# Bias row sums, operand loads further ahead and a denser row order in a two-layer graph kernel

## The chip, the cores and the metric

The kernel runs on one core of one Trainium2 chip. The metric is the device time of one execution in microseconds. A profiled execution, taken by the hardware profiler, shows where that time goes; inside it, times are counted from the start of its span. All matrix work is in 32-bit floats, and the trace shows every such matmul as two records: a 128x512 matmul is two records that start 0.43 us apart.

## The reference

N is 4096 nodes, D is 512 features, H is 128 hidden features. The first layer is attention with the adjacency matrix added twice to the scores, a residual and a layer norm; the second is a two-layer graph convolution with a residual and a layer norm.

```python
q = x @ Wq.T + bq;  k = x @ Wk.T + bk;  v = x @ Wv.T + bv
a = q @ k.T / sqrt(D) + adj + adj
x = layernorm(x + softmax(a) @ v)
h = relu(adj @ (x @ W1) + b1)
out = layernorm(x + adj @ (h @ W2) + b2)
```

The biases bq, bk, bv, b1 and b2 are not zero.

## The kernel before

All five engines run one instruction stream each, in the order in which the Python code calls them. The order is written out by hand; waits come from data dependences and from buffers that are used again. DMAs are issued by SyncE (SP), ScalarE (ACT) and GpSimd (POOL), each from its own in-order queue.

**Head** (lines 608 to 677). q k^T is computed as x M x^T plus bias terms, where M is Wq^T Wk times a scale. The head loads the transposed weights (wq_t on ACT's queue, wk_t on SP's), turns them back with TensorE transposes (psw), and computes M (psm). The bias terms are matmuls too: bk spread over 128 columns (bk_b) times Wq gives g_t in every row (psg); bk_b times bq gives the constant c0_t (psc); Wk times bq, one column at a time, gives ub_t (psub). Then row_parts computes one number per node, the sum of x times g, as a VectorE multiply with a running sum, and add_c0 adds the constant. The helpers spread (put a column on a diagonal, VectorE) and in_every_row (a matmul of ones with that diagonal, then a copy by ACT) turn a column into a row that stands in all 128 partitions. u_products (psu) multiplies M with x^T, and its result plus ub_t is the right operand of the scores.

**Row stages.** Queries are taken in NG = 8 groups of 512 columns. The unit loop issues, for each group g, the score products (qk, lines 346 and following, by a seven-product Strassen scheme) and, woven between them, a list of further work: for the group before it, the products P x (px_items, line 482, again seven products per block, each a *phase*) and, for the group before that, the rows (row_items): rows_out multiplies with Wv, adds the residual and starts the layer norm; rows_norm applies it on ACT; add_b2 adds b2 on POOL into a tile xb and stores it to x1_d; project turns the row tile (x1ps, copied to x1t), and project2 multiplies it with W1 (tps). Every gap between two score products takes items from the list until its share of the time is used up. The last group's P x has no scores beside it.

Each phase needs a left operand from x (plain parts, from the input) or from xs_d (sums that were stored before); load_x fetches it on SP into one of three buffers of the pool xnp. It is called at the start of phase n for phase n + 2. SP also loads the score operands (load_s), into the pool sap of eight buffers, which the xb tiles of add_b2 share.

**Second layer.** adj times the node features runs in four Strassen blocks (b, line 851, its right operands prepared by VectorE from the adjacency tiles ck), then a plain product for the last 1024 columns in three parts of 512, 256 and 256 (acce, line 1123). Adjacency tiles are loaded by SP (load_to, line 792), up to ten tiles ahead in the last part. During the last block and the parts, out_row finishes output rows: a matmul with W2 (ops), an addition of the x1 row (xp, loaded in pairs by load_pair on ACT's queue, two pairs ahead, four buffers), a layer norm, and a store on ACT's queue.

Of the kernel before, what the change touches and what calls it, by code (L numbers as in the profile page):

```python
# [24 lines left out]
def tile_graph_attention_then_gcn(  # L25
# [380 lines left out]

    def load_x(n):
        g, a, b, k = PHASES[n]
        XN[n] = xnp.tile([P, b - a, 2 * P], F32, tag="xn", name=f"xn{n}")
        plain = {1: (0, 0), 2: (1, 0), 4: (1, 1)}  # L410
        if k in plain:
            t, f = plain[k]
            src = x.rearrange("(d t j p) f -> t p d j f", p=P, t=2, j=2)[t]
            for d in range(a // 2, b // 2):
                nc.sync.dma_start(
                    XN[n][:, 2 * d - a : 2 * d - a + 2], src[:, d, :, ts(f, 2 * P)]
                )
        else:
            nc.sync.dma_start(XN[n], xs_d[a][:, {6: 0, 7: 1, 3: 2, 5: 3}[k]])
# [47 lines left out]
    def px_items(g):  # L467
        def one(n, q, f):
            _, a, b, k = PHASES[n]

            def go():
                if q == a and f == 0:
                    if n + 2 < len(PHASES):
                        load_x(n + 2)
                    if k in (6, 5, 3, 4):
                        read_px(("PY",) if k == 4 else ("PX",))
                    if k == 1 and a == 0:
                        OT[g] = rowp.tile([P, ND, W], F32, tag="ot", name=f"ot{g}")
                    if k in (1, 2, 7):
                        T["PX" if k == 1 else "PY"] = bank("o", f"p{n}", 4)  # L480
                begins = k in (1, 2, 7) and q == a
                nc.tensor.matmul(  # L482
                    T["PX" if k in (1, 6, 5, 3) else "PY"][:, ts(f, HW)],
                    XN[n][:, q - a, ts(f, P)],
                    quarters(g, q)[{1: 0, 2: 2, 6: 1, 7: 0, 5: 1, 4: 2, 3: 3}[k]],
                    start=begins and f == 0,
                    stop=q == b - 1,
                    skip_group_check=True,
                )
                if f == 1:  # L490
                    if k == 6:
                        px_t34(g, q)
                    if k == 7:
                        px_t1(g, q)
                    if q == b - 1:
                        px_read(g, a == 0, k)

            return PX_US, go

        return [  # L500
            one(n, q, f)
            for n, (g_, a, b, k) in enumerate(PHASES)
            if g_ == g
            for q in range(a, b)
            for f in range(2)
        ]
# [74 lines left out]
    def row_items(g, between):  # L581

        def item(us, f, *args):
            return us, lambda: f(*args)

        def out(r):
            return [item(0.86, rows_out, g, r, c) for c in range(ND)]

        def norm(r):
            return [item(0, rows_norm, g, r), item(0, add_b2, g, r)]

        def pro(r):
            return [item(0.44, project, g, r)]

        def pro2(r):
            return [item(0.9, project2, g, r)]

        w = between  # L600
        return [
            *out(0), *out(1), *out(2), *norm(0), *out(3), *norm(1), *w(4), *norm(2), *pro(0),
            *w(8), *norm(3), *pro(1), *pro2(0), *w(8), *pro(2), *pro2(1), *w(8), *pro(3),
            *pro2(2), *w(8), *pro2(3),
        ]


    with tc.tile_pool(name="wqk", bufs=1) as wp:
        wk_t = wp.tile([P, ND, D], F32, name="wk_t")
        wq_t = wp.tile([P, ND, D], F32, name="wq_t")  # L610
        wk_n = wp.tile([P, ND, D], F32, name="wk_n")
        wq_n = wp.tile([P, ND, D], F32, name="wq_n")
        bk_b = wp.tile([P, ND, P], F32, name="bk_b")

        nc.scalar.dma_start(wq_t, wqT.rearrange("(c p) o -> p c o", p=P))
        nc.sync.dma_start(wk_t, wkT.rearrange("(c p) o -> p c o", p=P))
        make_identity(nc, ident)
        nc.gpsimd.memset(ones, 1.0)
        nc.gpsimd.memset(half_t, -0.5)
        nc.scalar.dma_start(bq_t, bq)  # L620
        nc.scalar.dma_start(bk_t, bk)
        load_xts(0)
        rows0 = t_sb[:, : PER * PER, :].rearrange("p (r a) b -> p r (a b)", r=PER)
        nc.sync.dma_start(rows0, x[:W, :].rearrange("(r p) d -> p r d", p=P))
        load_xts(1)
        for i in range(4):
            nc.gpsimd.dma_start(
                b1_t[ts(i // 2, H // 2), i % 2 : i % 2 + 1], b1[ts(i % 2, H // 2), :]
            )
        for o in range(ND):  # L630
            nc.vector.tensor_scalar(bk_b[:, o, :], ones, bk_t[:, o : o + 1], None, ALU.mult)

        def evict(n, out_, in_):
            if n % 2:
                nc.vector.tensor_copy(out_, in_)
            else:
                nc.scalar.copy(out_, in_)


        for w_t, w_n in ((wq_t, wq_n), (wk_t, wk_n)):  # L640
            for o in range(ND):
                ps = bank("o", f"psw{o}", 4)
                for c in range(ND):
                    nc.tensor.transpose(ps[:, ts(c, P)], w_t[:, c, ts(o, P)], ident)
                evict(o, w_n[:, o, :], ps)
        ps = mbank("psg")
        for o in range(ND):
            nc.tensor.matmul(ps, bk_b[:, o, :], wq_n[:, o, :], start=o == 0, stop=o == ND - 1)
        nc.vector.tensor_scalar(g_t, ps, HALF_SCALE, None, ALU.mult)

        for a in range(ND):
            ps = bank("o", f"psm{a}", 4)
            for o in range(ND):
                nc.tensor.matmul(
                    ps, wq_n[:, o, ts(a, P)], wk_n[:, o, :], start=o == 0, stop=o == ND - 1
                )
            evict(a, m_t[:, a, :], ps)
        ps = mbank("psc")
        for o in range(ND):
            nc.tensor.matmul(  # L660
                ps[:, :1], bk_b[:, o, :], bq_t[:, o : o + 1], start=o == 0, stop=o == ND - 1
            )
        nc.vector.tensor_scalar(c0_t, ps[:, :1], HALF_SCALE, None, ALU.mult)
        ps = mbank("psub")
        for a in range(ND):
            for o in range(ND):
                nc.tensor.matmul(
                    ps[:, a : a + 1],
                    wk_n[:, o, ts(a, P)],
                    bq_t[:, o : o + 1],  # L670
                    start=o == 0,
                    stop=o == ND - 1,
                )
        nc.vector.tensor_scalar(ub_t, ps[:, :ND], HALF_SCALE, None, ALU.mult)
        for r in range(PER):
            row_parts(r, rows0[:, r, :])
        add_c0(0)

    SLOTS = 12

# [242 lines left out]
    for g in range(NG):  # L923
# [30 lines left out]
                px.insert(40 + 29 * n, (0.86, lambda u=u, k=k: product(u, k)))  # L954
        if g:
            px.reverse()
            items = row_items(g - 1, lambda n: [px.pop() for _ in range(n)])
            work[s1 + 1] = NP, items + px[::-1]
        else:
            work[s1 + 3] = NP - 2, px  # L960

    at(NP + 2, 3, load_x, 0)
    at(NP + 2, 5, load_x, 1)

    last_unit = (NG + 1) * NP + 1
    at(last_unit - 5, 0, lambda: [sum_t(0, 0, 8), sum_t(8, 8, 14)])
# [6 lines left out]
    for unit in range(last_unit):  # L973
        if unit == NP + 2:
# [4 lines left out]
            wv_t = wvp.tile([P, ND, D], F32, name="wv_t")  # L979
            w1_t = wvp.tile([P, ND, H], F32, name="w1_t")  # L980
            rowp = att.enter_context(tc.tile_pool(name="rows", bufs=1, side="right"))
        if unit == NP + 6:
            nc.sync.dma_start(wv_t, wvT.rearrange("(c p) o -> p c o", p=P))
            nc.sync.dma_start(w1_t, w1.rearrange("(c p) h -> p c h", p=P))
# [46 lines left out]
    def last_pools():  # L1031
        att.close()
        return [
            ctx.enter_context(tc.tile_pool(name=name, bufs=bufs, side="right"))
            for name, bufs in (("hp", 1), ("cp", 1), ("yp", 4), ("rows1", 4), ("small1", 4))
        ]

    put(61, lambda: pools.extend(last_pools()))
# [35 lines left out]
    def load_pair(i):  # L1074
        if i < NT // 2:
            XP[i] = rowp.tile([P, 2, D], F32, tag="x1", name=f"xp{i}")
            nc.scalar.dma_start(XP[i], x1_d[i])

    def out_row(uT, i):

        if i % 2 == 0:
            load_pair(i // 2 + 2)
        ps = mbank(f"ops{i}")
        nc.tensor.matmul(ps, uT, w2_t, start=True, stop=True)  # L1084
        y = XP[i // 2][:, i % 2]
# [16 lines left out]
            out_row(*pending.pop(0))  # L1102

    put(0, rows_of, 2, C[2])
    put(1, load_pair, 0)
    put(1, load_pair, 1)
    for n in range(18, 54, 6):
        put(n, some_rows, 1)
    strassen(3, beside)
# [3 lines left out]
    for n, (i0, cols, ld) in enumerate(parts):  # L1113
        acc = bank("o", f"acce{n}", 4)[:, :cols]
        per = 2048 // cols
        for j in range(NT):
            if j % (2 * per) == 0:
                load_to((ld + j // per) // 2 + 5)
            if n == 0 and j == 0:
                rows_of(3, C[3])  # L1120
            if j % (2, 5, 10)[n] == 1:
                some_rows(1)
            nc.tensor.matmul(  # L1123
                acc,
# [3 lines left out]
                stop=j == NT - 1,  # L1128
            )
        uT = yp.tile([P, cols], F32, tag="y", name=f"uTe{n}", padded_shape=[P, 1024])  # L1130
        nc.scalar.copy(uT, acc)
        pending += [(uT[:, ts(r, P)], i0 // P + r) for r in range(cols // P)]
    some_rows(len(pending))

# [42 lines left out]
```

## Time and profile before

| | |
|---|---|
| three runs | 2392.92, 2397.09 and 2399.93 us; median 2397.09 |
| profiled execution | 2397.79 us, span 2395.8 us, mean granted TensorE clock 0.994 |
| busy | PE 97%, VectorE (DVE) 66%, GpSimd (POOL) 42%, ACT 16% |
| moved | 522.98 MB, 218 GB/s on average |

Four views are used. The page gives the share of each engine. The list of waits names for an engine the line that waited, who released it, the total, the number of times and the longest. The timeline shows instructions in order of time: start, duration, engine, line, operation, out<-in, shapes, count, and in brackets the engine's idle time before it with what ended that. A table of windows gives the busy time per engine in stretches of the span, with the clock that TensorE was granted, the share of time that the DMA engines were busy, and GB/s. PEld is TensorE's weight load, which overlaps the matmuls.

### The profile page before, as it was taken

Reading aid. Unit: us, or ns where it says so; the run is one execution under the profiler, and the core shown is the slowest. Engines: PE = TensorE matmul, PEld = TensorE weight load, DVE = VectorE, ACT = ScalarE, POOL = GpSimd, SP = SyncE. Lnnn points to the kernel's source line nnn. Section 1 sums busy time; section 2 is a strip of 40 time slices with the busy share of each in tenths; the row PEclk is TensorE's granted clock in tenths of the full one; section 3 lists DMA queues with packets and bytes.
Section 4 is the critical chain, followed back from the end, with each engine's and each line's share of the span. In section 5 each row is a group of like instructions: output and inputs, shape, how many; then the busy total and the mean of one; then the engine's idle time right before and its main releaser. Section 6 shows DMA issues by size and latency. Waiting matters only on the chain.

```text
span 2395.8 us, 27767 instructions
## 1 busy us (share of the span) xinstructions
PE 2323.8 (97%) x10352; PEld 1705.7 (71%) x10352; DVE 1579.3 (66%) x2205; ACT 385.1 (16%) x398; POOL 1004.9 (42%) x1004
## 2 busy tenths in 40 slices
PE   8999899999999999999999999999998999999997
PEld 4666678878878887888788788878886743333445
DVE  2556665577568666765775576667657777888863
ACT  1111211031112112210311121121102100000012
POOL 0666554174237424541752274246429830001032
PEclk9999999999999999999999999999999999999999
DMA  4789877856766784768567667857664468999995
GB/s 140 236 266 301 243 207 189 231 159 189 206 171 179 206 220 141 206 186 230 145 196 208 171 172 199 221 151 202 181 203 153 144 233 311 332 350 333 356 384 182
DMA packets 271460, 522.98 MB, mean 218 GB/s; under 512 B 19104, under 2 KB 119968, under 8 KB 270432
## 3 DMA queue, kind: packets, MB, share of 16 engines
q1 hardware_dynamic: 223088, 404.81, 50.8%
q0 software_dynamic: 39872, 97.00, 19.2%
q10 hardware_dynamic: 8368, 19.41, 2.3%
q8 instruction: 83, 1.36, 0.2%
q14 instruction: 49, 0.40, 0.1%
HBM read 473.18 MB, written 46.40 MB: 217 GB/s over the span
## 4 chain that ended last, share of the span: by engine, by line
PE 87%; DVE 6%; DMA 3%; POOL 2%; issue 2%; ACT 0%; SPq 0%; POOLq 0%; DVEq 0%; ACTq 0%
PE p L482 29%; PE X L346 17%; PE b L851 14%; PE Y L346 13%; PE x L545 4%; PE psu L168 4%; PE acce L1123 2%; DVE s L435 2%; DVE s L440 1%; DMA xn<-in_x_dram 1%; PE ops L1084 1%; PE tps L576 1%; DVE s L359 1%; DMA ck<-in_adjT_dram 1%; DMA s<-in_adjT_dram 1%
## 5 line engine op out<-in xcount | busy, mean ns | idle before, releaser
L482 PE MATMUL p<-s,xn 128*128 128x256 f32 x3584 | 895.4, 381 | 34.5 <-DMA xn<-in_x_dram 12.1
L482 PEld LDWEIGHTS p<-s,xn 128*128 128x128 f32 x3584 | 678.4, 190 | 142.2 <-issue 13.7
L346 PE MATMUL X<-ut,sa 128*128 128x256 f32 x1984 | 515.0, 383 | 5.1 <-DVE s L359 5.1
L346 PEld LDWEIGHTS X<-ut,sa 128*128 128x128 f32 x1984 | 373.1, 191 | 108.2 <-issue 43.3
L402 POOL TENSOR_TENSOR lacc<-lacc,s 128x512 f32<-128x512 f32 x240 | 351.6, 1465 | 201.2 <-ACT s L393 191.4
L359 DVE TENSOR_TENSOR s<-X,s 128x512 f32<-128x512 f32 x256 | 176.4, 689 | 365.2 <-PE X L346 355.8
L346 PE MATMUL Y<-ut,sa 128*128 128x256 f32 x1408 | 361.0, 379 | 3.2 <-DVE s L359 1.8
L346 PEld LDWEIGHTS Y<-ut,sa 128*128 128x128 f32 x1408 | 266.3, 190 | 63.4 <-issue 25.6
L393 ACT ACTIVATE s<-s 128x1024 f32<-128x1024 f32 x128 | 135.4, 1058 | 863.4 <-DVE s L389 863.4
L292 POOL DMA_DIRECT2D s<-in_adjT_dram x64 | 86.7, 1355 | 413.7 <-ACT s L287 413.7
L359 DVE TENSOR_TENSOR s<-Y,s 128x512 f32<-128x512 f32 x192 | 132.1, 688 | 184.5 <-PE Y L346 184.4
L389 DVE TENSOR_TENSOR s<-s,mb 128x512 f32<-128x512 f32 x256 | 233.3, 917 | 0.0
L368 DVE TENSOR_TENSOR macc<-macc,s 128x512 f32<-128x512 f32 x240 | 226.6, 944 | 1.2
L526 POOL TENSOR_SCALAR rstd<-mv 128x1 f32<-128x1 f32 x64 | 26.4, 412 | 460.6 <-DVE mv L524 459.9
L455 DVE TENSOR_TENSOR ot<-p,ot 128x512 f32<-128x512 f32 x248 | 168.8, 681 | 28.6 <-PE p L482 27.8
L818 DVE TENSOR_TENSOR tt<-ck 128x1024 f32<-128x1024 f32 x112 | 138.2, 1271 | 41.6 <-PE b L851 38.8
L851 PE MATMUL b<-tt,st 128*64 128x512 f32 (+1 forms) x768 | 156.1, 541 | 0.0
L435 DVE TENSOR_TENSOR s<-s 128x512 f32<-128x512 f32 x128 | 138.5, 1104 | 2.0 <-POOL s L429 2.0
L168 PE MATMUL psu<-xt,m_t 128*128 128x512 f32 x256 | 129.7, 600 | 0.0
L545 PE MATMUL x<-wv_t,ot 128*128 128x512 f32 x256 | 124.9, 597 | 1.1 <-DVE xr L550 0.9
L287 ACT COPY s<-cb 128x2048 f32<-128x2048 f32 x64 | 120.4, 1890 | 0.6
L428 POOL TENSOR_TENSOR s<-s 128x256 f32<-128x256 f32 x128 | 119.9, 937 | 0.6
(130 smaller groups left out, 1929.3 us busy)
## 6 DMA issues: line engine op xcount, KB each, us to landing
ck<-in_adjT_dram SPq DMA_DIRECT2D x128, 1024.0 KB, 7.2
s<-in_adjT_dram POOLq DMA_DIRECT2D x64, 1024.0 KB, 11.9
sa<-s_d SPq DMA_DIRECT2D x224, 256.0 KB, 5.6
xn<-in_x_dram SPq DMA_DIRECT2D x192, 256.0 KB, 3.5
xn<-xs_d SPq DMA_DIRECT2D x96, 512.0 KB, 4.9
sa<-in_xT_dram SPq DMA_DIRECT2D x168, 256.0 KB, 4.5
xn<-xs_d SPq DMA_DIRECT2D x64, 256.0 KB, 3.9
u_d<-uo POOLq DMA_DIRECT2D x7, 1792.0 KB, 7.4
```

The source lines that it names most:

```text
L168: nc.tensor.matmul(ps[o], m_t[:, c, ts(o, P)], XTS[b][:, c, :], start=c == 0, stop=c == ND - 1)
L346: nc.tensor.matmul(T["X" if k in (1, 6, 5, 3) else "Y"][:, ts(j, HW)], SA[g, d, a][:, c, j, :], UT[g, b][:, c, :], start=k in (1, 2, 7) an ...
L359: nc.vector.tensor_tensor(ck, ps, ck, ALU.add)
L368: nc.vector.tensor_tensor(MACC[g], MACC[g], ck[:, h, :], ALU.max)
L389: nc.vector.tensor_tensor(ck, ck, MB[g], ALU.subtract)
L402: nc.gpsimd.tensor_tensor(LACC[g], LACC[g], ck[:, h, :], ALU.add)
L435: nc.vector.tensor_tensor(b, b, t2, ALU.subtract)
L455: nc.vector.tensor_tensor(to, ps, to, ALU.add)
L482: nc.tensor.matmul(T["PX" if k in (1, 6, 5, 3) else "PY"][:, ts(f, HW)], XN[n][:, q - a, ts(f, P)], quarters(g, q)[{1: 0, 2: 2, 6: 1, 7: 0 ...
L545: nc.tensor.matmul(ps, OT[g][:, c, ts(r, P)], wv_t[:, c, :], start=c == 0, stop=c == ND - 1)
L818: nc.vector.tensor_tensor(t[:, :2], v[:, :, 1], v[:, 0], ALU.subtract)
L851: nc.tensor.matmul(BK[n][k][ts(half, HH)], lhs, right(u, i, half, b), start=q == 0, stop=q == NP - 1,)
```

## The change

There are five edits.

1. In the head, bk and bq are made into rows that stand in every partition (bk_r, bq_r), by two diagonals and two broadcasts ahead of the transposes. g, ub and c0 are then sums over a row: VectorE multiplies the loaded transposed weights with such a row and accumulates (times). g is turned into a row by a further diagonal and broadcast, after the second of four M products; c0, row_parts and add_c0 follow there. psg, psc, psub and bk_b go. The weights are loaded in halves, all on SP, wq first; bk and bq are first on ACT's queue.
2. load_x is called three phases ahead instead of two, with a fourth buffer (pool xnp2) for every fourth phase.
3. row_items takes another order: normalisations one row earlier, and two P x items between rows where there were four or eight. For the last group three times as many are taken.
4. x1 pairs are loaded by SP, four pairs ahead, with six buffers.
5. In the last three parts, the first output row of a part comes some tiles later, and VectorE instead of ACT copies the accumulated result (uTe).

```diff
-        XN[n] = xnp.tile([P, b - a, 2 * P], F32, tag="xn", name=f"xn{n}")
+        pool = xnp2 if n % 4 == 3 else xnp
+        XN[n] = pool.tile([P, b - a, 2 * P], F32, tag="xn", name=f"xn{n}")
...
-                    if n + 2 < len(PHASES):
-                        load_x(n + 2)
+                    if n + 3 < len(PHASES):
+                        load_x(n + 3)
...
-            *out(0), *out(1), *out(2), *norm(0), *out(3), *norm(1), *w(4), *norm(2), *pro(0),
-            *w(8), *norm(3), *pro(1), *pro2(0), *w(8), *pro(2), *pro2(1), *w(8), *pro(3),
-            *pro2(2), *w(8), *pro2(3),
+            *out(0), *out(1), *norm(0), *out(2), *norm(1), *out(3), *norm(2), *w(2), *pro(0),
+            *norm(3), *w(2), *pro(1), *w(2), *pro2(0), *w(2), *pro(2), *w(2), *pro2(1), *w(2),
+            *pro(3), *w(2), *pro2(2), *w(4), *pro2(3),
...
-        bk_b = wp.tile([P, ND, P], F32, name="bk_b")
-        nc.scalar.dma_start(wq_t, wqT.rearrange("(c p) o -> p c o", p=P))
-        nc.sync.dma_start(wk_t, wkT.rearrange("(c p) o -> p c o", p=P))
+        bq_r = wp.tile([P, W], F32, name="bq_r")
+        bk_r = wp.tile([P, W], F32, name="bk_r")
+        g_c = wp.tile([P, ND], F32, name="g_c")
+        nc.scalar.dma_start(bk_t, bk)
+        nc.scalar.dma_start(bq_t, bq)
+        for w_t, wT in ((wq_t, wqT), (wk_t, wkT)):
+            for o in range(2):
+                nc.sync.dma_start(
+                    w_t[:, :, ts(o, D // 2)],
+                    wT.rearrange("(c p) o -> p c o", p=P)[:, :, ts(o, D // 2)],
+                )
...
-        nc.scalar.dma_start(bq_t, bq)
-        nc.scalar.dma_start(bk_t, bk)
...
-        for o in range(ND):
-            nc.vector.tensor_scalar(bk_b[:, o, :], ones, bk_t[:, o : o + 1], None, ALU.mult)
...
+        def times(w_t, b_r, into):
+            product = t_sb[:, 24 : 24 + PER, :].rearrange("p a b -> p (a b)")
+            for c in range(into.shape[1]):
+                nc.vector.scalar_tensor_tensor(
+                    product, w_t[:, c, :], HALF_SCALE, b_r, ALU.mult, ALU.mult,
+                    accum_out=into[:, c : c + 1],
+                )
+        for name, b_t, b_r in (("bk", bk_t, bk_r), ("bq", bq_t, bq_r)):
+            spread(b_t, name)
+            in_every_row(name, b_r)
...
-        ps = mbank("psg")
-        for o in range(ND):
-            nc.tensor.matmul(ps, bk_b[:, o, :], wq_n[:, o, :], start=o == 0, stop=o == ND - 1)
-        nc.vector.tensor_scalar(g_t, ps, HALF_SCALE, None, ALU.mult)
+        times(wq_t, bk_r, g_c)
+        spread(g_c, "g")
+        times(wk_t, bq_r, ub_t)
...
-        ps = mbank("psc")
-        for o in range(ND):
-            nc.tensor.matmul(
-                ps[:, :1], bk_b[:, o, :], bq_t[:, o : o + 1], start=o == 0, stop=o == ND - 1
-            )
-        nc.vector.tensor_scalar(c0_t, ps[:, :1], HALF_SCALE, None, ALU.mult)
-        ps = mbank("psub")
...
-        nc.vector.tensor_scalar(ub_t, ps[:, :ND], HALF_SCALE, None, ALU.mult)
-        for r in range(PER):
-            row_parts(r, rows0[:, r, :])
-        add_c0(0)
+            if a == 1:
+                in_every_row("g", g_t)
+                times(bq_r.unsqueeze(1), bk_r, c0_t)
+                for r in range(PER):
+                    row_parts(r, rows0[:, r, :])
+                add_c0(0)
...
-            items = row_items(g - 1, lambda n: [px.pop() for _ in range(n)])
+            by = 3 if g == NG - 1 else 1
+            items = row_items(g - 1, lambda n: [px.pop() for _ in range(n * by)])
...
-    at(NP + 2, 5, load_x, 1)
+    at(NP + 2, 4, load_x, 1)
+    at(NP + 2, 5, load_x, 2)
...
+            xnp2 = att.enter_context(tc.tile_pool(name="xnp2", bufs=1, side="right"))
...
-            for name, bufs in (("hp", 1), ("cp", 1), ("yp", 4), ("rows1", 4), ("small1", 4))
+            for name, bufs in (("hp", 1), ("cp", 1), ("yp", 4), ("rows1", 6), ("small1", 4))
...
-            nc.scalar.dma_start(XP[i], x1_d[i])
+            nc.sync.dma_start(XP[i], x1_d[i])
...
-            load_pair(i // 2 + 2)
+            load_pair(i // 2 + 4)
...
-    put(1, load_pair, 0)
-    put(1, load_pair, 1)
+    for i in range(4):
+        put(1, load_pair, i)
...
-            if j % (2, 5, 10)[n] == 1:
+            if j % (2, 5, 10)[n] == (1, 3, 4)[n]:
...
-        nc.scalar.copy(uT, acc)
+        nc.vector.tensor_copy(uT, acc)
```

More of the change, by code (lines that the diff above doesn't have):

```diff
@@ L637, in evict @@
                 nc.scalar.copy(out_, in_)
+        def times(w_t, b_r, into):
+            product = t_sb[:, 24 : 24 + PER, :].rearrange("p a b -> p (a b)")
+            for c in range(into.shape[1]):
+                nc.vector.scalar_tensor_tensor(
+                    product,
+                    w_t[:, c, :],
+                    HALF_SCALE,
+                    b_r,
+                    ALU.mult,
+                    ALU.mult,
+                    accum_out=into[:, c : c + 1],
[3 more added lines that the diff above has]
+            in_every_row(name, b_r)
         for w_t, w_n in ((wq_t, wq_n), (wk_t, wk_n)):
@@ L657, in tile_graph_attention_then_gcn @@
             evict(a, m_t[:, a, :], ps)
-        ps = mbank("psc")
-        for o in range(ND):
-            nc.tensor.matmul(
-                ps[:, :1], bk_b[:, o, :], bq_t[:, o : o + 1], start=o == 0, stop=o == ND - 1
-            )
-        nc.vector.tensor_scalar(c0_t, ps[:, :1], HALF_SCALE, None, ALU.mult)
-        ps = mbank("psub")
[L665 to L673, printed above, removed]
-        nc.vector.tensor_scalar(ub_t, ps[:, :ND], HALF_SCALE, None, ALU.mult)
-        for r in range(PER):
-            row_parts(r, rows0[:, r, :])
-        add_c0(0)
+            if a == 1:
[4 more added lines that the diff above has]
+                add_c0(0)
     SLOTS = 12
```

## The prediction

> **What bounds the kernel now.** First the busy shares and the granted clock on the page:
>
> ```profile
> span 2395.8 us, 27767 instructions
> PE 2323.8 (97%) x10352; PEld 1705.7 (71%) x10352; DVE 1579.3 (66%) x2205; ACT 385.1 (16%) x398; POOL 1004.9 (42%) x1004
> PEclk9999999999999999999999999999999999999999
> ```
>
> TensorE works 97% of the span. Work taken off VectorE or GpSimd is worth nothing by itself; only PE's instructions, or the 72 us in which PE idles, can be won. So the second view is what PE waits for:
>
> ```profile
> PE p L482 <- DMA xn<-in_x_dram: 12.1, 6, 2.7
> PE psw L644 <- DMA wq_t<-in_wqT_dram: 10.7, 1, 10.7
> PE p L482 <- DVE ot L455: 7.4, 7, 1.5
> PE ops L1084 <- DVE xp L1086: 6.3, 2, 4.4
> PE p L482 <- DVE s L435: 5.6, 5, 1.6
> PE ops L1084 <- ACT uTe L1131: 2.2, 2, 1.8
> PE p L482 <- DMA xn<-xs_d: 1.7, 2, 1.4
> ```
>
> (total, times, longest.) The third is the timeline of the start, for PE work that could go:
>
> ```profile
> 10.74 3.31 PE L644 MATMUL psw<-ident,wq_t 128*128 128x128 f32 x16 [10.74 <-DMA wq_t<-in_wqT_dram]
> 13.89 1.97 PE L644 MATMUL psw<-ident,wk_t 128*128 128x128 f32 x16
> 15.69 3.60 PE L648 MATMUL psg<-wq_n,bk_b 128*128 128x512 f32 x8
> 19.12 13.90 PE L654 MATMUL psm<-wk_n,wq_n 128*128 128x512 f32 x32
> 32.86 0.95 PE L660 MATMUL psc<-bq_t,bk_b 128*128 128x1 f32 x8
> 33.67 3.71 PE L667 MATMUL psub<-bq_t,wk_n 128*128 128x1 f32 x32
> 37.24 5.38 PE L168 MATMUL psu<-xt,m_t 128*128 128x512 f32 x8
> ```
>
> PE starts at 10.7 us, and psg, psc and psub run one after another ahead of psu. The windows show one thing more (length, then PE, PEld, DVE, ACT, POOL busy, PE clock, DMA share, GB/s):
>
> ```profile
> 33.00:37.30 4.30, 4.30 (x42) 4.30 (x40) 0.85 (x2) 0.00 (x0) 0.00 (x0) 1.00 0.00 0
> 37.30:41.30 4.00, 4.00 (x7) 1.70 (x7) 3.71 (x11) 0.00 (x0) 0.00 (x0) 0.57 0.31 68
> ```
>
> After the one-column psub the granted clock was 0.57.
>
> **Head.** Removed from PE: psg 3.44, psc and psub 4.38 (32.86 to 37.24). Added: three 128x512 broadcasts of 0.86 (the bcc row: two records, 0.43 apart), two of them ahead of the transposes. *Loads:* wq and wk now go in four halves on SP, bk and bq first on ACT. Before, wq (9.9 us to landing) shared the engines with wk; SP's four 1 MB loads landed at 9.5, 12.8, 15.3 and 17.9, 2.5 to 3.3 us apart, and the rate was 362 to 369 GB/s from 3 us on. So the 0.5 MB halves land near 4.3, 5.8, 7.4 and 9.0. A rule speaks against this: the Trainium skill, "DMA: Bandwidth & Descriptors" (Anatomy of one DMA), puts 2.0 us plus bytes at 436 GB/s on a DMA, and its Bandwidth section asks for 1 MiB each. My estimate from it, one after another: 3.2 us a half, the last at 13.5. That would start psm near 14.5 and cost 2.5 us. The trace shows loads queued on SP landing with no such gap, so I take 9.0. *Biases:* bq and bk landed 0.8 us apart behind wq; the quietest x1 load took 2.0. At the queue's front that gives about 3.6 and 4.4. The other end is the b_t row, tiny loads on a queue of their own, 6.5 us: 7.2 and 7.8. I take the former, since it is these very loads. Then the diagonal on DVE (0.69) and the broadcasts: at half clock 1.72 each, from 4.5 to 7.9. The skill's "TensorE: Matmul & The Clock Gate" (Part 1) says PE begins at half clock until some 3.4 us of activity, and falls back after as long idle. That speaks against work put at the front: full clock would give 0.86 each. The trace agrees, with 3.31 for the first 16 transposes against 1.97 for the next, so I charge the half clock; it costs 1.7 us at most. Transposes (1.73 for sixteen, the wk row) 7.9 to 9.7 and, wk being there, to 11.4; with slack, psm from 12 (11.5 to 15 by the biases' ends), plus 13.73 plus 0.86: psu at 26.6 against 37.24, so 10.6. The slow stretch goes too: the first eight psu records took 5.24 in the chain, where eight at 0.43 are 3.44: 1.8. Sum 12.4; I take **12** (9 to 13).
>
> On DVE nine row sums of 0.69 + 0.08 (the L325 rows) and three diagonals replace six small operations. Four sums and a diagonal, 3.8, must be done before the g broadcast, which stands behind two psm groups (6.9): 3 us of cover. ub (3.1) and c0 with row_parts (about 4.8) lie beside the rest of psm, whose second half is 6.9. Were that cover gone, at most 3 us would show. ACT gains three copies of 0.59 while idle.
>
> **Three ahead.** In each of six row stages PE waits once for an xn tile, 1.3 to 2.7 us. The cause stands in SP's own waits between 685 and 770 us and in its timeline there:
>
> ```profile
> SPq L254 <- DMA x_d<-xb: 11.9, 1, 11.9
> 723.24 0.32 SPq L419 DMA_DIRECT2D xn<-xs_d  x1
> 735.50 0.32 SPq L254 DMA_DIRECT2D sa<-s_d  x1
> 735.92 0.40 SPq L415 DMA_DIRECT2D xn<-in_x_dram  x1
> 739.74 0.67 PE L482 MATMUL p<-s,xn 128*128 128x256 f32 x2 [1.60 <-DMA xn<-in_x_dram]
> ```
>
> An sa load waits 12 us for a buffer that an xb row holds until its store lands, and the xn load behind it on the in-order SP queue is late. A fourth buffer puts that load one phase (3 to 6 us) earlier, ahead of the hold or with more time behind it; the denser order also brings xb forward and puts P x phases some 4 us later just there. The next load is late then, but has a phase more: landing takes 3.5, it is due about 6 us after 736. Six waits: 1.34 + 1.60 + 2.40 + 2.68 + 1.91, and 2.50 at 1403 in the same place, put down to an ACT copy long done: **12.4**. The first stage loses its 2.2 and 0.2, **2.4** (low end 0, if the copies of wv in the queue still delay it).
>
> **Denser rows** change no PE work; 18 instead of 36 P x items lie between row items, and the rest run later, all together. Costs come from tighter order. On ACT the third and fourth normalisations now come right after their matmuls and may wait for POOL; behind them stand the x1t and ot copies, on which the next transposes and phases wait, with 1.6 us (two items at the stage's pace of 1.84) of cover for a 0.59 copy. On PE, P x without rows between begins 11 us earlier. The nearest row is the stage's own rowless stretch, with one wait of 1.0 per stage (ot L455). The upper bound is stage 0, dense throughout: 1.35 + 0.83 + 1.58 = 3.8 per stage, 23 in all; below nothing, those 5.9 of ot waits and 1.9 of s waits could also vanish. I take half a wait a stage: **+3**.
>
> **Last row stage** (no QK). Its 11.5 of idle is POOL and DVE preparing P x, 1.4 is xn. Three times the items between rows leave phases at nearly the same places (k=6 due 17.6 us in, both ways), but xb of row 1 (1.27 + 0.3 + 0.67) moves ahead of the P x subtraction that PE awaits at 1812 for 2.9 us: +2. Net **+0.6** (-4 to +4).
>
> **Tail.** Two waits come from late x1 rows and one from the uTe copy:
>
> ```profile
> 2331.63 1.12 PE L1084 MATMUL ops<-w_t,y 128*128 128x512 f32 x2 [1.81 <-DVE xp L1086]
> 2345.47 0.69 DVE L1086 TENSOR_TENSOR xp<-ops,xp 128x512 f32<-128x512 f32 x1 [7.72 <-DMA xp<-x_d]
> 2346.22 2.07 PE L1084 MATMUL ops<-w_t,y 128*128 128x512 f32 x2 [4.45 <-DVE xp L1086]
> 2369.93 1.12 PE L1084 MATMUL ops<-w_t,uTe 128*128 128x512 f32 x2 [1.79 <-ACT uTe L1131]
> ```
>
> Four pairs ahead give 20.6 us (eight rows of 2.57) instead of 10.3. Now SP: a load waits for the stores of the pair six before it, and ck loads queue behind; and it queues behind ck loads that wait for slots. At the first part's start eight ck loads are issued at once, the last held until tile 7 is used, 10 us; the x1 load behind lands after some 17, in time. ck is ten tiles ahead there, so the reverse hold (2 to 3 us) is covered. The uTe copy on DVE takes 0.69 or 0.42 and the first row now stands three tiles later: 1.8 gained. Against it: 2 MB of x1 instead of 1.5 stand early in the last Strassen block, where DMA already runs at 400 GB/s and DVE waited 2.1 for ck with some 1.3 of slack to PE: 0.5 MB is 1.3 us, so I charge 1.2 (0 to 6). **6.3 + 1.8 - 1.2 = 6.9.**
>
> **Sum.** 12 + 2.4 + 12.4 - 3 - 0.6 + 6.9 = 30.1. The profiled execution took 2397.8 (its span and 2.0 around it): 2367.7. It stands 0.7 above the median of the three runs, hence **2367**.
>
> **Rivals.** *The stall moves:* dense phases and ACT's earlier waits eat the row stages' gain (9.4) and cost 2.4 more in the last: 2379. For it speaks stage 0; against it that DVE has a third of its time free. *Biases late:* psm at 15 or later, and the tail's gain halved: 2367 + 3 + 3.5 = 2374. For it speaks the b_t row. *SP's queue decides (the slower side):* in the last block ten x1 loads each wait for an out store (5.7 us to landing) and hold the ck loads behind; of these 57 us the refill at the part's start covers 10, so 47 are lost on top of 2367: 2414. It ends slower once over 3 us a load show on PE (30 won, ten loads). Against it: ck's lead, and no PE wait for ck now. *It does nothing:* each wait is followed by another of its size, 2397; against it, psg, psc and psub are PE work that is gone.
>
> **Numbers.** Likeliest 0.66, its own range 2357 to 2377; stall moves 0.17, biases 0.09, SP 0.05, nothing 0.03. Faster by over 0.3% (7.2 us; the runs span 2392.9 to 2399.9, so less is not told from no change) 0.91, within 0.04, slower 0.05. The range for 8 in 10 takes in the first rival and the bounds: 2354 to 2384.
>
> **What would show it.** psu from 25 to 30 us with no window at 0.57; no PE wait for xn above 1 us in the six stages; no wait of ops for xp; new waits of x1ps or tps, or more of ot, would be the dense rows' price. It is wrong if psm starts after 16, if p waits grow past 12 in the six stages, or if b or acce waits for ck.

## The result, and the profile after

The changed kernel took 2366.97 us (median of four runs, 2365.97 to 2367.78), the kernel before 2398.4 in its four runs beside it (2392.92 to 2399.93): a ratio of 0.9873, with a 95% interval of 0.9856 to 0.989. The predicted time was 2367. But two parts of that sum are wrong by 5.7 and by 7.0 us in opposite directions. That they cancel is luck, so the number says less for the reasoning than it seems to.

The page's first rows after. TensorE is again the engine that is nearly always busy; VectorE is busy 13 us longer than before:

```profile
span 2365.5 us, 27707 instructions
PE 2313.5 (98%) x10310; PEld 1697.6 (72%) x10310; DVE 1592.0 (67%) x2222; ACT 383.5 (16%) x398; POOL 1011.4 (43%) x1004
```

Next, from the list of TensorE's waits over the whole span after, the rows used below (waiting line and its releaser; total, times, longest):

```profile
PE p L483 <- DVE s L436: 8.1, 10, 1.9
PE ops L1094 <- DVE xp L1096: 8.1, 2, 7.5
PE X L346 <- DVE s L359: 8.0, 18, 1.0
PE bcbk L315 <- DVE diagbk L304: 4.9, 1, 4.9
PE p L483 <- POOL s L430: 3.5, 1, 3.5
...
PE p L483 <- POOL xb L560: 2.4, 1, 2.4
...
PE p L483 <- DVE ot L456: 1.5, 2, 1.0
...
PE ops L1094 <- DVE uTe L1141: 0.5, 1, 0.5
```

The wait for xn is gone, the start waits 4.9 us instead of 10.7, and the ot waits (7.4) are down to 1.5. Others have grown. ops waits for xp 7.5 us at once where the two waits before were 6.3 together. The waits for s that VectorE prepares went from 5.6 to 8.1 (p) and from 5.1 to 8.0 (X), and p has a new wait of 2.4 for xb.

To see where the time went, cut both spans at the same instructions. Every row is the distance between two first occurrences in the two timelines (first psu at 37.24 and 26.34, first score matmul at 53.61 and 40.94, the mt transpose of group 1 at 465.29 and 449.31, that of the last stage at 1785.17 and 1754.12, the first x matmul of the last group's rows at 1933.89 and 1903.94, the first acce at 2297.38 and 2268.18, the end at 2395.8 and 2365.5):

| Stretch | before | after | gain | predicted |
|---|---|---|---|---|
| head, to the first score | 53.61 | 40.94 | 12.7 | 12 |
| first stage | 411.68 | 408.37 | 3.3 | 2.4 |
| six middle row stages | 1319.88 | 1304.81 | 15.1 | 12.4 - 3 = 9.4 |
| last row stage | 148.72 | 149.82 | -1.1 | -0.6 |
| Strassen blocks to the first part | 363.49 | 364.24 | -0.8 | -1.2 |
| the parts, to the end | 98.42 | 97.32 | 1.1 | 6.3 + 1.8 = 8.1 |
| sum | | | 30.3 | 30.1 |

The head in the timeline after (start, duration, engine, line, operation, out<-in, shapes, count, idle before it and what ended that):

```profile
4.92 2.04 PE L315 MATMUL bcbk<-diagbk,ones 128*128 128x512 f32 x2 [4.92 <-DVE diagbk L304]
6.76 1.66 PE L315 MATMUL bcbq<-diagbq,ones 128*128 128x512 f32 x2
8.26 1.91 PE L666 MATMUL psw<-ident,wq_t 128*128 128x128 f32 x16
10.00 1.91 PE L666 MATMUL psw<-ident,wk_t 128*128 128x128 f32 x16
11.75 7.03 PE L675 MATMUL psm<-wk_n,wq_n 128*128 128x512 f32 x16
18.62 1.02 PE L315 MATMUL bcg<-diagg,ones 128*128 128x512 f32 x2
19.48 7.03 PE L675 MATMUL psm<-wk_n,wq_n 128*128 128x512 f32 x16
26.34 3.60 PE L168 MATMUL psu<-xt,m_t 128*128 128x512 f32 x8
```

The two broadcasts take 2.04 and 1.66 where the one for g takes 1.02: the slow first microseconds of TensorE now fall on two matmuls (four records), and the sixteen transposes behind them need 1.91 instead of 3.31. The granted clock reads 1.00 from 4.90 to 8.26 us, so this slowness shows in the durations alone. The broadcast of g stands in the middle of psm with no wait. The first eight psu records take 3.60 instead of 5.38.

The tail after, around the one long wait:

```profile
2253.77 36.26 SPq L799 DMA_DIRECT2D ck<-in_adjT_dram  x10
2290.12 4.22 SPq L1087 DMA_DIRECT2D xp<-x_d  x2
2302.11 0.69 DVE L1096 TENSOR_TENSOR xp<-ops,xp 128x512 f32<-128x512 f32 x1 [11.92 <-DMA xp<-x_d]
2302.86 2.07 PE L1094 MATMUL ops<-w_t,y 128*128 128x512 f32 x2 [7.54 <-DVE xp L1096]
```

SP issues ten ck loads over 36 us and only then comes to the next x1 pair, which lands 12 us later. TensorE stands for 7.54 us and then is slow. The windows say how slow (length; PE, PEld, DVE, ACT, POOL busy; granted clock; DMA share; GB/s):

```profile
2300.00:2302.80 2.80, 0.00 (x0) 0.00 (x0) 0.69 (x1) 0.00 (x0) 0.00 (x0) 0.50 1.04 380
2302.80:2306.20 3.40, 3.34 (x4) 1.50 (x5) 3.09 (x8) 0.81 (x1) 1.60 (x5) 0.50 1.09 349
2306.20:2310.00 3.80, 3.80 (x7) 1.57 (x6) 1.31 (x3) 1.63 (x2) 1.54 (x5) 0.68 1.06 385
```

At 0.50 and 0.68 these 7.2 us do 4.3 us of work: the wait costs 2.9 more than its own length.

### The profile page after: what moved, and what is told of

Read it like the earlier page. It is cut to its first block, busy times and chain, and to the rows that moved or that the text cites. A ratio compares the mean times of both kernels' runs of the same rounds, so it can differ in the third digit from the quotient of the medians.

```text
span 2365.5 us, 27707 instructions
## 1 busy us (share of the span) xinstructions
PE 2313.5 (98%) x10310; PEld 1697.6 (72%) x10310; DVE 1592.0 (67%) x2222; ACT 383.5 (16%) x398; POOL 1011.4 (43%) x1004
## 4 chain that ended last, share of the span: by engine, by line
PE 90%; DVE 6%; issue 1%; DMA 1%; POOL 1%; ACT 0%; DVEq 0%; POOLq 0%; ACTq 0%
PE p L483 30%; PE X L346 17%; PE b L858 14%; PE Y L346 13%; PE x L546 4%; PE psu L168 4%; PE acce L1133 2%; DVE s L436 2%; PE tps L577 1%; PE ops L1094 1%; DVE s L359 1%; DVE s L441 1%; DMA s<-in_adjT_dram 1%; PE x1ps L568 1%; PE psm L675 1%
## 5 line engine op out<-in xcount | busy, mean ns | idle before, releaser
L389 DVE TENSOR_TENSOR s<-s,mb 128x512 f32<-128x512 f32 x256 | 244.1, 957 | 0.0
L429 POOL TENSOR_TENSOR s<-s 128x256 f32<-128x256 f32 x128 | 125.4, 980 | 0.6
```

Of the source, the lines that this page charges most:

```text
L389: nc.vector.tensor_tensor(ck, ck, MB[g], ALU.subtract)
```

## The experiments

Each of the first seven takes back one part of the change, or tests one suspected cause, by itself. The runs of the kernel before that stand beside them have medians of 2396.89 (x1_act, own_xb, old_rows and xn_two) and 2396.43 (the other four), seven runs each.

**x1_act: x1 on ACT's queue, otherwise the changed kernel.**

```diff
-            nc.sync.dma_start(XP[i], x1_d[i])
+            nc.scalar.dma_start(XP[i], x1_d[i])
```

> The changed kernel, with the x1 pairs loaded by ACT's queue again, still four pairs ahead with six buffers. Theory A (the 7.5 us wait of ops at 2303 us comes from x1 loads standing on SP's in-order queue behind ten ck loads, which take 26 us at 390 GB/s): on a queue of their own they share the engines with ck and arrive in time; ops waits for xp fall below 2 us in all, 2367.0 becomes about 2360. Theory B (the DMA engines are simply full there, at 390 GB/s, whichever queue a load stands on): the wait stays at 6 to 8 us, the time within 1.5 us of 2367. A third outcome, waits of b or acce for ck, would mean that x1 takes ck's place.

Measured: 2357.62 us (2356.82 to 2358.89), ratio 0.984 (0.9823 to 0.9856). From the first acce to the end it takes 87.78 us instead of 97.32, and every other stretch stays within 1.5 us of the changed kernel's. TensorE's waits in that stretch, all of them:

```profile
PE ops L1094 <- DVE cl L875: 1.1, 1, 1.1
PE ops L1094 <- DVE uTe L1141: 0.5, 1, 0.5
```

So the four pairs' lead is worth 9.5 us more than the changed kernel got, and SP's queue is what took it away. Against the kernel before the parts gain 10.6 here: more than the 8.1 of idle time that the prediction had counted. The windows over the parts, before and then in x1_act, show where the rest is:

```profile
2297.00:2396.00 99.00, 82.23 (x250) 47.41 (x244) 41.45 (x82) 22.45 (x29) 27.15 (x78) 0.95 0.74 258
2267.00:2355.00 88.00, 78.13 (x244) 46.03 (x244) 43.95 (x86) 21.15 (x26) 27.15 (x78) 0.98 0.81 287
```

TensorE is also busy 4.1 us less, at a mean clock of 0.98 instead of 0.95. Before, the 4 us after the wait of 4.45 ran at 0.50 and the next 4 at 0.81, which is 2.8 us lost.

**x1_act2: x1 on ACT's queue and only two pairs ahead, with four buffers**, so that of the change in the parts only the row places and the uTe copy remain.

```diff
-            for name, bufs in (("hp", 1), ("cp", 1), ("yp", 4), ("rows1", 6), ("small1", 4))
+            for name, bufs in (("hp", 1), ("cp", 1), ("yp", 4), ("rows1", 4), ("small1", 4))
...
-            nc.sync.dma_start(XP[i], x1_d[i])
+            nc.scalar.dma_start(XP[i], x1_d[i])
...
-            load_pair(i // 2 + 4)
+            load_pair(i // 2 + 2)
...
-    for i in range(4):
-        put(1, load_pair, i)
+    put(1, load_pair, 0)
+    put(1, load_pair, 1)
```

> The changed kernel, with x1 pairs on ACT's queue and two pairs ahead with four buffers, as before; the row places and the copy of uTe stay as changed. x1_act (four ahead on ACT) gave 2357.6. Theory A (the lead is worth what the prediction said, two late rows, 6.3 us and the half-clock stretch after each): the waits of ops for xp return, 6 us in all, 2364 to 2367. Theory B (the queue alone decides, lead is without effect): no ops wait above 1 us, 2357 to 2359.

Measured: 2367.03 us (2364.99 to 2368.24), ratio 0.9865 (0.9846 to 0.9884), which is the time of the changed kernel. In its timeline both waits of before are back:

```profile
2302.50 1.12 PE L1094 MATMUL ops<-w_t,y 128*128 128x512 f32 x2 [1.74 <-DVE xp L1096]
...
2317.62 2.08 PE L1094 MATMUL ops<-w_t,y 128*128 128x512 f32 x2 [4.11 <-DVE xp L1096]
```

Before, they were 1.81 and 4.45. The parts take 96.13 us, 2.3 less than before, and that is what the later rows and the uTe copy give. Four pairs ahead on SP's queue (97.32, the changed kernel) are worth nothing beside two on ACT's (96.13); four on ACT's (87.78) are worth 8.3 more.

**own_xb: the kernel BEFORE, with xb in a pool of its own** instead of in a buffer that the sa loads wait for; two phases ahead and the old row order stay.

```diff
-        xb = sap.tile([P, D], F32, tag="sa", name=f"xb{g}_{r}")
+        xb = xbp.tile([P, D], F32, tag="xb", name=f"xb{g}_{r}")
...
+            xbp = att.enter_context(tc.tile_pool(name="xbp", bufs=2, side="right"))
```

> The kernel before, with one edit: the xb tiles of add_b2 have two buffers of their own instead of sharing the sap pool with the score operands. Theory A (SP is held by score loads that wait for a buffer taken by xb, and xn loads stand behind them): the SP waits for x_d<-xb go from 74.7 us to near 0, the six waits for xn in the row stages (12.4 us) vanish although loads are still two phases ahead, and the time is 2398 less 9 to 13, about 2387. Theory B (the xn loads are late for want of lead or bandwidth, whatever holds SP): the six waits stay, the time within 3 us of before.

Measured: 2382.78 us (2381.78 to 2386.33), ratio 0.9946 (0.993 to 0.9961). The six middle stages take 1304.60 us, 15.3 less than before and as little as in the changed kernel. TensorE's waits within 470 to 1774 us:

```profile
PE p L482 <- DVE ot L455: 6.7, 6, 1.1
PE X L346 <- DVE s L359: 1.9, 6, 0.3
```

No wait for xn is left, and little has taken its place: the ot waits were 5.9 there before. SP's waits for the stores of xb, 74.7 us before, are gone altogether. This shows the cause which the prediction read from SP's waits: the sa load that waits for xb's buffer holds up the xn load behind it.

**old_rows: the row order of before, with three phases ahead.**

```diff
-            *out(0), *out(1), *norm(0), *out(2), *norm(1), *out(3), *norm(2), *w(2), *pro(0),
-            *norm(3), *w(2), *pro(1), *w(2), *pro2(0), *w(2), *pro(2), *w(2), *pro2(1), *w(2),
-            *pro(3), *w(2), *pro2(2), *w(4), *pro2(3),
+            *out(0), *out(1), *out(2), *norm(0), *out(3), *norm(1), *w(4), *norm(2), *pro(0),
+            *w(8), *norm(3), *pro(1), *pro2(0), *w(8), *pro(2), *pro2(1), *w(8), *pro(3),
+            *pro2(2), *w(8), *pro2(3),
...
-            by = 3 if g == NG - 1 else 1
+            by = 1
```

> The changed kernel, with the row order of before in all stages. The six middle stages gained 15.1 us (31.05 at the last stage against 15.98 after the first), of which 12.4 were waits for xn. Theory A (denser rows cost, as the prediction had it, 3 us): 2364. Theory B (they gain what is over, by taking the ot waits of about 1 us a stage away): the ot waits of 0.9 to 1.2 us at some 75 us into each stage return and the time is 2370 to 2374. In the last stage the order of before should take back 1.1 us of loss.

Measured: 2366.68 us (2365.47 to 2367.96), ratio 0.9876 (0.9861 to 0.9891): the changed kernel's time. Neither number expected came: the rows' order costs nothing in the whole. Its six stages take 1304.14 us, so three phases ahead alone give 15.7. Beside the changed kernel that is 0.7 less, which is not told from scatter: the five kernels with the denser order and three phases ahead take 1304.14 to 1304.81 there, the two with the old order (old_rows and best) 1304.14 and 1304.71. The last row stage takes 148.75 (changed kernel 149.82, before 148.72), so the 1.1 lost there is the denser order's: the six kernels that have it take 149.57 to 149.82, the four with the old order 148.40 to 148.75. It does not show in the medians.

**xn_two: the new row order, with two phases ahead.**

```diff
-        pool = xnp2 if n % 4 == 3 else xnp
-        XN[n] = pool.tile([P, b - a, 2 * P], F32, tag="xn", name=f"xn{n}")
+        XN[n] = xnp.tile([P, b - a, 2 * P], F32, tag="xn", name=f"xn{n}")
...
-                    if n + 3 < len(PHASES):
-                        load_x(n + 3)
+                    if n + 2 < len(PHASES):
+                        load_x(n + 2)
...
-    at(NP + 2, 4, load_x, 1)
-    at(NP + 2, 5, load_x, 2)
+    at(NP + 2, 5, load_x, 1)
```

> The changed kernel, with load_x two phases ahead and three buffers again; all else as changed, the denser rows too. Theory A (the third phase ahead is what removed the six waits for xn): they return, 1.3 to 2.7 us each or more since SP is now held for some 21 us a stage (127 us over six stages), so 12 to 20 us slower than 2367, at 2379 to 2387. Theory B (the denser order removed them, by moving P x later past the hold): at most 4 us slower, 2371.

Measured: 2372.23 us (2370.89 to 2374.73), ratio 0.99 (0.9885 to 0.9916), 5.3 above the changed kernel. The loss of 12 to 20 us that theory A expects did not come; B is nearer. The six stages take 1306.35 us, 13.5 less than before and only 1.5 more than with three ahead. TensorE's waits within 452 to 1759 us:

```profile
PE X L346 <- DVE s L359: 4.0, 12, 0.4
PE p L482 <- DMA xn<-xs_d: 3.4, 5, 1.2
```

The waits for xn are still there but shrunk, five of at most 1.2. The denser order alone does most of the cure that the prediction put down to the third phase. It does not do so by freeing SP, whose waits for the stores of xb grew from 74.7 to 126.6 us; that it moves the P x phases past the hold is the likely reason, which no run shows by itself. Another 3.1 us lie in the first stage, which takes 411.51, as before: what the third phase adds to the denser order is the first stage's 3.1 and 1.5 in the six.

**psub_back: the psub matmuls in place of ub's row sums.**

```diff
-        times(wk_t, bq_r, ub_t)
...
+        ps = mbank("psub")
+        for a in range(ND):
+            for o in range(ND):
+                nc.tensor.matmul(
+                    ps[:, a : a + 1],
+                    wk_n[:, o, ts(a, P)],
+                    bq_t[:, o : o + 1],
+                    start=o == 0,
+                    stop=o == ND - 1,
+                )
+        nc.vector.tensor_scalar(ub_t, ps[:, :ND], HALF_SCALE, None, ALU.mult)
```

> The changed kernel, with ub computed on TensorE again: the 32 one-column psub matmuls after psm, in place of the four row sums. Theory A (they cost their own 3.6 us and leave the clock at half for the first psu, 1.8 us): 2367.0 + 5.4 = 2372.4, with psu near 30 us, a granted clock below 0.7 in the 4 us after it starts, and eight psu records in 5 us or more. Theory B (the slow psu of before had another cause, the wait for ub or the weight loads): 2370.6 at most, full clock after psub.

Measured: 2374.4 us (2373.25 to 2375.51), ratio 0.9896 (0.9877 to 0.9915), 7.4 above the changed kernel: theory A's direction, and more than it asked. Its timeline:

```profile
26.76 4.56 PE L687 MATMUL psub<-bq_t,wk_n 128*128 128x1 f32 x32
31.18 6.10 PE L168 MATMUL psu<-xt,m_t 128*128 128x512 f32 x8
```

Its windows over these psu and a little ahead of them:

```profile
30.00:34.00 4.00, 4.00 (x11) 2.45 (x11) 2.61 (x5) 0.00 (x0) 0.00 (x0) 0.50 0.25 91
34.00:38.00 4.00, 4.00 (x9) 1.68 (x8) 0.05 (x1) 0.68 (x2) 0.00 (x0) 0.74 0.46 171
```

The sixteen one-column matmuls (32 records) take 4.4 us by themselves (26.76 to 31.18) and leave TensorE at half clock: the next eight psu records take 6.10 instead of 3.60. Together with 0.4 by which psub starts later than psu did this is 7.3 at the first score (48.27 against 40.94).

**wq_whole: wq and wk as whole 1 MB loads on two queues**, bk and bq still first.

```diff
-        for w_t, wT in ((wq_t, wqT), (wk_t, wkT)):
-            for o in range(2):
-                nc.sync.dma_start(
-                    w_t[:, :, ts(o, D // 2)],
-                    wT.rearrange("(c p) o -> p c o", p=P)[:, :, ts(o, D // 2)],
-                )
+        nc.scalar.dma_start(wq_t, wqT.rearrange("(c p) o -> p c o", p=P))
+        nc.sync.dma_start(wk_t, wkT.rearrange("(c p) o -> p c o", p=P))
```

> The changed kernel, with wq as one 1 MB load on ACT's queue (behind the biases) and wk as one on SP's, as before; all else as changed. Theory A (what counts is that wq comes first and alone): wq shares the engines with wk and lands near 10.7, psm starts near 14.4 instead of 11.75, and 2.7 us are lost, 1.3 more if the clock falls back meanwhile: 2369.7 to 2371. Theory B (a load's fixed cost makes whole loads better than halves): psm at 11.75 or earlier, 2367 or less.

Measured: 2372.9 us (2371.1 to 2375.09), ratio 0.989 (0.9871 to 0.991), 5.9 above the changed kernel. wq landed 11.9 us after its issue and wk 6.0; in the changed kernel the halves of wq landed 4.0 and 5.0 after theirs and those of wk 6.9 and 8.0. The timeline:

```profile
13.68 3.67 PE L662 MATMUL psw<-ident,wq_t 128*128 128x128 f32 x16 [3.03 <-DMA wq_t<-in_wqT_dram]
17.15 2.68 PE L662 MATMUL psw<-ident,wk_t 128*128 128x128 f32 x16
19.67 7.03 PE L671 MATMUL psm<-wk_n,wq_n 128*128 128x512 f32 x16
```

The tensor that is needed first lands last, and behind the gap of 3.03 the transposes are slow again (3.67 and 2.68 for sixteen, against 1.91). psm starts 7.9 us later; 2.5 of that are the slow transposes (13.68 to 19.67, against 8.26 to 11.75). The edit changes the size of the loads and wq's queue at once, and with that the order of landing. Whole loads on SP alone, wq first, were not run, so the loss is not shown to come from the size.

**best: all that these runs speak for in one kernel**, the changed one with x1 on ACT four pairs ahead, xb in its own pool and the row order of before.

```diff
-            nc.sync.dma_start(XP[i], x1_d[i])
+            nc.scalar.dma_start(XP[i], x1_d[i])
...
-        xb = sap.tile([P, D], F32, tag="sa", name=f"xb{g}_{r}")
+        xb = xbp.tile([P, D], F32, tag="xb", name=f"xb{g}_{r}")
...
-            by = 3 if g == NG - 1 else 1
+            by = 1
```

(with row_items as in old_rows and the pool xbp as in own_xb)

> The changed kernel, with x1 on ACT's queue four pairs ahead, the row order of before in all stages, and two buffers of their own for xb. x1_act gave 2357.6; the old order stood 0.7 us better over the six middle stages and 1.1 in the last; own xb buffers end the SP holds, which cost PE nothing any more with three phases ahead. If the terms add: 2355 to 2357. If the denser order pays once SP is not held: 2358 or more.

Measured: 2357.11 us (2355.03 to 2357.69), ratio 0.9823 (0.98 to 0.9845). That beats both kernels and is not told apart from x1_act's 2357.62. The six stages take 1304.71 us (x1_act 1304.76), the last row stage 148.40 (149.70). Once no xn load is late, freeing the sa buffers adds nothing: the three cures of the middle stages overlap.

## Why the prediction was right, and where it was not

**What bounds it: right.** Every gain lies in removed TensorE work, removed TensorE waits or the slow clock behind them. Whether any of VectorE's 13 us of longer busy time shows is not separated: TensorE's waits for s grew by 5.4 and those for ot shrank by 5.9.

**Head, 12: right in its steps.** The chosen landings of the biases (3.6 and 4.4) put the broadcasts at 4.5 to 7.9; they ran from 4.92 to 8.26. Both biases landed later, near 4.1 and 5.8 us, and the slow first broadcast hid most of the second's delay. The halves of the weights were 0.4 to 1.3 later too, which the slack took up. psm was to start at 12 and started at 11.75, psu at 26.6 and started at 26.34. The slow stretch after psub, charged at 1.8, is worth 1.8: from the first psu to the first score before 16.37, after 14.60. psub_back shows both its parts. One window after answers the one at 0.57 before:

```profile
26.30:30.30 4.00, 4.00 (x11) 1.80 (x10) 3.18 (x5) 0.32 (x1) 0.00 (x0) 1.00 0.39 142
```

Between the rule and the row on the halves, the row was the right choice. From "DMA: Bandwidth & Descriptors" in the Trainium skill (Anatomy of one DMA) I had estimated psm near 14.5; it started at 11.75. That section gives its sum for DMAs which GpSimd issues, and these are issued by SP; to put four of them one after another was my own step. The four halves, issued within 2.1 us, landed 4.0, 5.0, 6.9 and 8.0 us after their issues, so they overlapped. Its Bandwidth section, which asks for 1 MiB a load, would have spoken for wq_whole, which is 5.9 slower; there the order of landing changed together with the size.

**Three ahead, 12.4, and denser rows, +3: cause right, sizes wrong.** own_xb shows the cause, and it shows that curing it is worth 15.3. Two steps failed. The first: the six waits were charged at their idle time. The window over the six stages before (length; busy time of PE, PEld, DVE, ACT, POOL with counts; clock; DMA share; GB/s):

```profile
465.00:1785.00 1320.00, 1299.52 (x5909) 1092.83 (x5908) 874.45 (x1220) 235.47 (x225) 597.86 (x568) 1.00 0.68 186
```

The same window after, with the same 5909 matmuls:

```profile
449.00:1754.00 1305.00, 1296.22 (x5909) 1090.15 (x5908) 882.99 (x1220) 233.54 (x225) 605.24 (x568) 1.00 0.68 188
```

Idle time falls by 11.7 (20.48 to 8.78) and busy time by 3.3 besides. Windows of the kernel before, just after the waits of 2.68 and 2.50 us, show where most of the 3.3 comes from:

```profile
1181.50:1185.50 4.00, 3.96 (x12) 3.33 (x13) 1.59 (x1) 1.06 (x1) 3.84 (x4) 0.65 0.78 240
1403.50:1407.50 4.00, 4.00 (x18) 3.31 (x19) 2.65 (x4) 1.06 (x1) 3.84 (x4) 1.00 0.83 273
```

After two of the six waits (1181 and 1623 us) the clock was 0.65 and 0.63 for 4 us, which is 1.4 and 1.5 us lost; after the other four it was full. The second step: "half a wait a stage" for the denser rows, 3 us, was at most 0.7 in six stages, and may be nothing. The ot waits went (6.7 in old_rows to 1.0), and waits of s at 0.7 or less and of X at 0.4 or less came in their place. The prediction had allowed for that as the lower end and took a middle value, with no row behind it but stage 0, whose other work differs. It also gave the third phase the credit for a stall that the denser order by itself nearly ends (xn_two, 13.5 of 15.1).

**Last row stage, +0.6: right in sign**, 1.1. Two gaps of the stage after:

```profile
1778.89 1.41 PE L483 MATMUL p<-s,xn 128*128 128x256 f32 x4 [2.36 <-POOL xb L560]
1783.84 2.07 PE L483 MATMUL p<-s,xn 128*128 128x256 f32 x4 [3.54 <-POOL s L430]
```

xb does stand ahead of the subtraction that TensorE awaits; that wait grows from 2.9 to 3.54, and the trace puts a further one of 2.36 down to xb itself. Others shrank, so that the stage idles 11.9 us against 11.7 before; most of the 1.1 is longer busy time, at a mean clock of 0.97 against 0.99.

**Tail, 6.9: the step that failed.** The prediction said "eight ck loads are issued at once, the last held until tile 7 is used, 10 us", and that the x1 load behind them "lands after some 17, in time". It came to be issued 22 us after the first part began (2268.18 to 2290.12) and landed at 34. The step counted buffers, and the traffic points to the transfers as the bound. The DMA view from 2253 to 2290 us:

```profile
DMA packets 7766, 13.99 MB, mean 378 GB/s; under 512 B 386, under 2 KB 2009, under 8 KB 7764
...
ck<-in_adjT_dram SPq DMA_DIRECT2D x10, 1024.0 KB, 13.5
```

The first line is the traffic of all queues, the second the ck issues (number, size, median us to landing). In these 37 us ten loads of 1 MB and 3.5 MB of other traffic went through, and SP was no faster than that with its issues. The lead in ck was hardly there to be drawn on: the DMA engines were as full in the Strassen block before (405 GB/s from 2230 to 2268 us, busy share 1.03). Dividing bytes by the rate of 380 GB/s would have warned of it. By such an estimate the eight ck loads of the prediction need 22 us with the engines to themselves, and 29 with the share that ck had here (10.5 of 14 MB), where the prediction had 10 to 17. What it is that keeps SP from issuing further ahead stays open. SP's waits from 2205 to 2330 us name stores, ck loads and matmuls in turn:

```profile
SPq L799 <- DMA out_dram<-xp: 22.4, 5, 6.9
SPq L799 <- DMA ck<-in_adjT_dram: 16.7, 8, 3.3
SPq L799 <- PE acce L1133: 6.5, 3, 3.2
```

and no run separates them. So the full engines are shown, and that they alone set SP's pace is not. On ACT's queue (x1_act) about the same bytes move in the same 37 us (14.10 MB), but an x1 pair lands 7.6 us after its issue (median) and does not stand behind the ck loads. The 1.8 for uTe is borne out by its wait, now 0.5 at VectorE, and by the 2.3 of x1_act2. The charge of 1.2 for the earlier x1 loads came out at 0.8 here, but old_rows has the same loads and lost nothing (363.48): the five kernels with four pairs ahead on SP take 363.5 to 366.5 there, all the others 363.5 to 363.7.

**The rivals.** "SP's queue decides" had the right mechanism and the wrong direction: what reached TensorE is the x1 load that waits behind ck, not ck behind x1, and in the changed kernel TensorE never waited for ck. It cost 9.5 of the tail and did not turn the sign. The biases were not late enough to hold up psm. In the middle stages the waits for s and X grew by 5.2 us, about what those for ot lost (4.9), so the stall for xn did not move there; and "does nothing" falls with the first row of the table.

## What to carry to other kernels

A load that is small and due soon does not go behind a stream that already runs at the DMA rate. Estimate its delay as the bytes in front divided by that rate, however many buffers are free. A longer lead on that queue gave nothing here; on another queue it gave 8.3 us. Charge a TensorE wait, or a run of one-column matmuls, with the slow clock that may follow as well as with its own length. Before adding two cures to one stall, ask whether either alone ends it: here each of three gave 13.5 to 15.7 us, and together no more.

## What was not expected of the hardware

- TensorE's granted clock fell to 0.63 and 0.65 over the 4 us after waits of only 1.91 and 2.68 us, and stayed at 1.00 after waits of 2.40 and 2.50. What tells these apart is not shown. The Trainium skill, "TensorE: Matmul & The Clock Gate" (Part 1), puts the fall at an idle window of some 3.4 us; here shorter waits sufficed, at times.
- One-column matmuls count as busy in the profile and still left the clock at 0.50 (psub_back, 30 to 34 us).
- The start of the kernel before is not the same each time: in own_xb, which doesn't touch it, the first score came at 57.80 instead of 53.61, with psub at 5.68 us and the psu behind it at 6.72. In the kernels without psub it lay between 40.8 and 43.8, but for wq_whole. So the gain of the head is some 4 us uncertain. That may be part of the scatter of the kernel before (2392 to 2404), which two profiles cannot show.
